# A router of two token tiles side by side: weights in halves of the array, tokens moving, logits turned once

## The chip, the cores and the metric

The kernel runs on one core of a Trainium2 chip. The metric is the device time in microseconds (us); three runs of the kernel before gave 1886.5, 1886.94 and 1890.55 us, with a median of 1886.94. The engines are PE (TensorE, with its weight loads listed apart as PEld), DVE (VectorE), ACT (ScalarE), POOL (GpSimd) and SP (SyncE, which here issues DMAs).

## The reference, cut to what matters

A decoder layer over x of 32 x 64 tokens of 512 numbers in float32: self attention of 32 heads of 128, a cross attention over the channels, and a mixture of biases of 64 experts, each behind a layer norm and each added to x. The change lies in the last:

```
def _L0_ffn_ref(hidden_states, router_weight, router_bias, expert_bias):
    K_TOP = 8
    ...
    flat = hidden_states.reshape(T, H)
    logits = jnp.einsum('th,eh->te', flat, router_weight) + router_bias
    scores = jax.nn.softmax(logits, axis=-1)
    topk_w, topk_idx = jax.lax.top_k(scores, K_TOP)
    w_sum = topk_w.sum(axis=-1, keepdims=True)
    w_dense = jnp.zeros((T, E), dtype=scores.dtype).at[jnp.arange(T)[:, None], topk_idx].add(topk_w)
    bias_mix = jnp.einsum('te,eh->th', w_dense, expert_bias)
    out = flat * w_sum + bias_mix
...
x = x + _L0_attn_ref(_layernorm(x, axis=-1), ...)
x = x + _L0_xattn_ref(_layernorm(x, axis=-1), ctx_1024, ...)
x = x + _L0_ffn_ref(_layernorm(x, axis=-1), ...)
```

T is 2048 tokens, H is 512 and E is 64.

## The kernel before, in words

The tokens are cut into 16 tiles of 128 (NT), so that a tile holds its tokens in the 128 partitions. The kernel has two phases. In the first, up to about 1400 us, the attention runs over groups of two heads (the functions of `HeadGroup` and `Window`, lines 363 to 815). In the second the attention's output is multiplied with Wo, two tiles (a pair) at a time, in seven products per pair instead of eight (`strassen_out`, line 947); a product is 16 matmuls of 128x256 on PE (`chunks`, line 847), and after every four of them the function yields.

At each yield the main loop calls `advance` (line 1449), which takes one step of every tile that has left the attention. Such a tile goes through `after_attention` (line 1187): first `cross_attention` (line 1057), then `experts` (line 1126). Both are generators; the number that they yield says how many further steps of four matmuls are let pass before they go on. So the work of a tile's tail is strewn between the output products of the next pair, and PE's order is exactly the order in which the code issues it (`manual_schedule` of PE, line 67). In this second phase the order of DVE, ACT, POOL and SP is not written out: the framework's scheduler chooses it, and the tile pools decide when a buffer may be written again.

The names that matter below:

- `transposed` (line 246) turns the four 128x128 blocks of a tile with four PE transposes (line 253), into PSUM.
- `experts`: layer norm `xn`; `ft`, the turned tile, copied from PSUM by ACT (line 1131); `pl`, the logits of 128 tokens by 64 experts, four matmuls that hold a block of 128 tokens as the weights and let the 64 columns of `rwt` stream (line 1135); `lg`, the logits with the bias (line 1139); `top`, `neg`, `ex`, `den`, `inv`, `rest`, `chosen`, the choice of the best eight and the softmax, on DVE, with the exponential on ACT (lines 1140 to 1153); `wd`, the dense weights, and `ws`, their sum (lines 1162 and 1164); line 1166 adds the tile times `ws` to x.
- Two tiles share one `wds`, and the second of them goes on: `pw` turns the dense weights of both at once (line 1173), `wt` is ACT's copy of it, `pm` is their product with the expert biases (line 1182), and line 1184 adds it to x, which is then stored. The last two tiles, 14 and 15, each go alone (`alone`).
- `cross_attention`: `kv` (lines 1067 and 1068), the energies `e` (line 1077: rows 0 to 63 and 64 to 127 of the array by turns), the softmax `probs` on DVE and ACT, `att` (line 1107, one buffer), their turned form, and `py` (lines 1112 and 1114, the latter into partitions 0 to 63 and 64 to 127 by turns), added at line 1122.
- `s` (line 559) are the scores of the first phase; they go to the two halves of the output partitions by turns.
- In the last pair of `strassen_out` (line 978) lines 1012, 1015 and 1016 add the last products to tile 15; line 229 is the statistics of a layer norm; lines 1024 to 1038 and 983 to 985 are DVE's sums over a whole block of 128x2048; lines 1042, 1045 and 1046 add products to `p1` and `p17`.

Of the kernel before, what the change touches and what calls it, by code (L numbers as in the profile page):

```python
# [8 lines left out]
F32 = mybir.dt.float32  # L9
AF = mybir.ActivationFunctionType  # L10
ALU = mybir.AluOpType
AX = mybir.AxisListType

P = 128
NB, SEQ, D = 32, 64, 512
NT = NB * SEQ // P
KC = D // P
# [11 lines left out]
NEXP = 64  # L29
# [12 lines left out]
def decoder_layer(  # L42
# [23 lines left out]
    nc = tc.nc  # L66
# [3 lines left out]
    small = ctx.enter_context(tc.tile_pool(name="small", bufs=4))  # L70
# [5 lines left out]
    ps_a = ctx.enter_context(tc.tile_pool(name="ps_a", bufs=3, space=bass.MemoryType.PSUM))  # L76
    ps_t = ctx.enter_context(tc.tile_pool(name="ps_t", bufs=2, space=bass.MemoryType.PSUM))
    ps_s = ctx.enter_context(tc.tile_pool(name="ps_s", bufs=3, space=bass.MemoryType.PSUM))
# [95 lines left out]
    def load_x(t, place=None):  # L174
# [9 lines left out]
        for q in range(NQUAD)  # L184
    ]

    ident = const.tile([P, P], F32, tag="ident", name="ident")
# [6 lines left out]
            name=nc.get_next_instruction_name(),  # L194
# [45 lines left out]
    def layernorm(xt, name):  # L240
        ((mean, rstd),) = statistics([xt], name, True)
        xn = work.tile([P, D], F32, tag="xn", name=f"xn_{name}", bufs=3)
        nc.vector.tensor_scalar(xn, xt, mean, rstd, ALU.subtract, ALU.mult)
        return xn

    def transposed(src, name, pool=None):

        if pool is None:
            pt = ps_t.tile([P, 4, P], F32, tag="pt", name=f"pt_{name}")
        else:  # L250
            pt = pool.tile([P, 4, P], F32, tag="ps", name=f"pt_{name}")
        for j in range(4):
            nc.tensor.transpose(pt[:, j, :], src[:, j, :], ident)  # L253
        return pt
# [869 lines left out]
    chosen_by = {}  # L1124

    def experts(t, xt):
        name = f"f{t}"
        xn = layernorm(xt, name)
        yield 3
        ft = work.tile([P, KC, P], F32, tag="ft", name=f"ft_{name}", bufs=1)  # L1130
        nc.scalar.copy(ft, transposed(xn.rearrange("p (kc k) -> p kc k", k=P), name))
        yield 1
        pl = ps_s.tile([P, NEXP], F32, tag="ps", name=f"pl_{name}")
        for kc in range(KC):
            nc.tensor.matmul(  # L1135
                pl, ft[:, kc, :], rwt[:, kc, :], start=kc == 0, stop=kc == KC - 1
            )
        lg = work.tile([P, NEXP], F32, tag="lg", name=f"lg_{name}")
        nc.vector.tensor_tensor(lg, pl, rb_b, ALU.add)
        top = small.tile([P, 8], F32, tag="top", name=f"top_{name}")  # L1140
        nc.vector.max(top, lg)
        neg = small.tile([P, 1], F32, tag="neg", name=f"neg_{name}")
        nc.vector.tensor_scalar(neg, top[:, 0:1], -1.0, None, ALU.mult)
        ex = work.tile([P, NEXP], F32, tag="ex", name=f"ex_{name}")
        den = small.tile([P, 1], F32, tag="den", name=f"den_{name}")
        nc.scalar.activation(ex, lg, AF.Exp, bias=neg, accum_out=den)
        inv = small.tile([P, 1], F32, tag="inv1", name=f"inv1_{name}")
        nc.vector.reciprocal(inv, den)

        rest = work.tile([P, NEXP], F32, tag="rest", name=f"rest_{name}")  # L1150
        nc.vector.match_replace(rest, top, lg, -3e38)
        chosen = work.tile([P, NEXP], F32, tag="chosen", name=f"chosen_{name}")
        nc.vector.tensor_tensor(chosen, lg, rest, ALU.not_equal)

        alone = t >= NT - 2
        side = 0 if alone else t % 2
        if side:
            wds, other = chosen_by.pop(t - 1)
        else:
            wds = work.tile([P, 2, NEXP], F32, tag="wds", name=f"wds_{name}")  # L1160
        wd = wds[:, side, :]
        nc.vector.scalar_tensor_tensor(wd, ex, inv, chosen, ALU.mult, ALU.mult)
        ws = small.tile([P, 1], F32, tag="ws", name=f"ws_{name}")
        nc.vector.tensor_reduce(ws, wd, AX.X, ALU.add)

        nc.vector.scalar_tensor_tensor(xt, xn, ws, xt, ALU.mult, ALU.add)
        if not alone and not side:
            chosen_by[t] = wds, xt
            return
        yield 3  # L1170
        n = NEXP if alone else 2 * NEXP
        pw = ps_t.tile([P, P], F32, tag="pt", name=f"pw_{name}")
        nc.tensor.transpose(pw[0:n, :], wds.rearrange("p a e -> p (a e)")[:, 0:n], ident)
        wt = work.tile([P, P], F32, tag="wt", name=f"wt_{name}")
        nc.scalar.copy(wt[0:n, :], pw[0:n, :])
        yield 1

        both = [(t, xt)] if alone else [(t - 1, other), (t, xt)]
        pms = [ps_a.tile([P, D], F32, tag="pa", name=f"pm{i}_{name}") for i in range(len(both))]
        for i, pm in enumerate(pms):  # L1180
            rows = slice(i * NEXP, (i + 1) * NEXP)
            nc.tensor.matmul(pm, wt[rows, :], eb_sb[rows, :], start=True, stop=True)
        for (at, it), pm in zip(both, pms):
            nc.vector.tensor_tensor(it, it, pm, ALU.add)
            nc.sync.dma_start(out=out_flat[bass.ts(at, P), :], in_=it)

    def after_attention(t, xt):
        second = t % 2 and t < NT - 1
        if second:
            yield 0  # L1190
        yield from cross_attention(t, xt, 3 if second else 1)
        yield from experts(t, xt)
# [13 lines left out]
    work = phase.enter_context(tc.tile_pool(name="attention", bufs=2))  # L1206
# [303 lines left out]
    work = ctx.enter_context(tc.tile_pool(name="output", bufs=2, reuse_waits="tile"))  # L1510
# [11 lines left out]
    rwt = work.tile([P, KC, NEXP], F32, tag="rwt", name="rwt", bufs=1)  # L1522
    load_beside(rwt, rw_t.rearrange("(kc p) e -> p kc e", p=P))
    rb_b = work.tile([P, NEXP], F32, tag="rb", name="rb_b", bufs=1)
# [76 lines left out]
```

## Time and profile before

| what | value |
| --- | --- |
| median of three runs | 1886.94 us |
| the profiled execution's own time | 1888.35 us |
| its span on the core | 1886.6 us |
| busy PE, share of the span | 1856.9 us, 98% |
| busy weight loads | 1613.8 us, 86% |
| busy DVE | 1259.9 us, 67% |
| busy ACT | 653.0 us, 35% |
| busy POOL | 1014.8 us, 54% |
| instructions | 40521 |

The span is the time from the first to the last instruction of the profiled execution; its own time has what lies around that. Busy times of PE are modelled where matmuls overlap, so the distance between two starts says more of a matmul's cost than its length does. "L1135 x8" in a row means eight instructions of line 1135; a float32 matmul appears as two passes, each with a weight load of its own. "128*64 128x128" is the part of the array in use (rows*columns) and what streams through it. An arrow to the left, as in "<-DVE xn_x L243", names what ended an engine's idle time.

### The profile page before, as it was taken

The numbers are of one execution on the slowest core, as the hardware profiler recorded it, in microseconds if no ns is written. First come the engines' busy times: TensorE is split into PE (matmuls) and PEld (weight loads), VectorE is DVE, ScalarE is ACT, GpSimd is POOL, SyncE is SP. The second block draws the span as 40 slices with busy tenths as digits, with TensorE's granted clock in tenths as the row PEclk, the third lists the DMA queues.
The fourth block names the chain that finished last, engine by engine and source line by source line (L and its number), as shares of the span: only waits on it lengthen the run. The fifth ranks groups of instructions, "written<-read, shape, count | busy, mean of one in ns | idle before, by whom it ended". The sixth has DMA issues, their size and how long they took to land.

```text
span 1886.6 us, 40521 instructions
## 1 busy us (share of the span) xinstructions
PE 1856.9 (98%) x16838; PEld 1613.8 (86%) x16838; DVE 1259.9 (67%) x2110; ACT 653.0 (35%) x1573; POOL 1014.8 (54%) x856
## 2 busy tenths in 40 slices
PE   9999999999999999999999999999999999999996
PEld 8888888888888888888888888888887888888884
DVE  6867777776777758776677677766684535554544
ACT  2344444344433443344433443443312211221122
POOL 5856776775667649776667767666241221121120
PEclk9999999999999999999999999999999999999997
DMA  4244434333443343333443333344844232223100
GB/s 141 68 132 145 129 121 128 124 108 124 127 131 104 113 147 102 113 102 114 131 129 113 113 113 102 102 135 135 299 137 154 70 114 80 80 71 115 45 26 23
DMA packets 164648, 215.04 MB, mean 114 GB/s; under 512 B 10160, under 2 KB 135152, under 8 KB 160368
## 3 DMA queue, kind: packets, MB, share of 16 engines
q1 hardware_dynamic: 157648, 206.62, 34.2%
q10 hardware_dynamic: 6816, 5.83, 1.0%
q8 instruction: 132, 2.16, 0.5%
q14 instruction: 52, 0.43, 0.1%
HBM read 172.05 MB, written 40.37 MB: 113 GB/s over the span
## 4 chain that ended last, share of the span: by engine, by line
PE 88%; DVE 5%; DMA 3%; POOL 2%; issue 1%; ACT 1%; ACTq 0%; SPq 0%; POOLq 0%; DVEq 0%
PE p_w L659 32%; PE py L852 17%; PE va L391 11%; PE vb L391 8%; PE ms_w L794 3%; PE o L596 3%; PE s L559 3%; PE pt_p L253 1%; PE pa L449 1%; PE e_x L1077 1%; PE py_x L1114 1%; PE py_x L1112 1%; PE pl_f L1135 1%; PE pt_x L253 1%; DMA rs<-row_w 1%
## 5 line engine op out<-in xcount | busy, mean ns | idle before, releaser
L659 PE MATMUL p_w<-x,w 128*128 128x256 f32 x2940 | 721.0, 382 | 3.6 <-DVE qk L670 2.9
L659 PEld LDWEIGHTS p_w<-x,w 128*128 128x128 f32 x2940 | 521.4, 190 | 60.2 <-DVE qk L670 2.4
L391 PEld LDWEIGHTS va<-w,x 128*128 128x128 f32 x2048 | 268.6, 192 | 13.0
L670 DVE TENSOR_TENSOR qk<-p_w,qk 128x512 f32<-128x512 f32 x360 | 213.1, 599 | 87.4 <-PE p_w L659 84.5
L391 PE MATMUL va<-w,x 128*128 128x128 f32 x2048 | 269.9, 275 | 0.0
L407 ACT COPY v<-va 128x256 f32<-128x256 f32 x256 | 96.2, 376 | 495.8 <-PE va L391 495.6
L683 DVE TENSOR_TENSOR qk<-p_w,qk 128x512 f32<-128x512 f32 x360 | 219.7, 620 | 40.5 <-PE p_w L659 36.8
L120 POOL TENSOR_TENSOR w<-w 128x768 f32<-128x768 f32 x126 | 243.9, 1946 | 2.4
L269 POOL TENSOR_TENSOR prob<-prob,inv 128x512 f32<-128x512 f32 x64 | 79.0, 1235 | 300.7 <-DVE inv L268 297.5
L546 POOL TENSOR_TENSOR qk<-qk,rs 128x512 f32<-128x512 f32 x128 | 177.8, 1390 | 105.9 <-DMA rs<-row_w 91.2
L852 PE MATMUL py<-wo,a 128*128 128x256 f32 x992 | 226.9, 381 | 0.0
L360 ACT ACTIVATE sq<-qk 128x512 f32<-128x512 f32 x256 | 161.4, 631 | 183.5 <-DVE qk L683 65.2
L852 PEld LDWEIGHTS py<-wo,a 128*128 128x128 f32 x992 | 184.3, 190 | 33.1 <-issue 8.7
L391 PEld LDWEIGHTS vb<-w,x 128*128 128x128 f32 x1536 | 201.4, 192 | 9.7
L391 PE MATMUL vb<-w,x 128*128 128x128 f32 x1536 | 202.4, 275 | 0.0
L548 DVE SCALAR_TENSOR_TENSOR qk<-qk,gqk,rs 128x512 f32<-128x512 f32 x128 | 181.6, 1419 | 4.2 <-DMA rs<-row_w 3.9
L852 PE MATMUL py<-wo_t,a 128*128 128x256 f32 x672 | 155.3, 382 | 0.0
L852 PEld LDWEIGHTS py<-wo_t,a 128*128 128x128 f32 x672 | 124.3, 190 | 17.6 <-issue 1.6
L976 POOL TENSOR_TENSOR x<-x,p 128x256 f32<-128x256 f32 x42 | 42.8, 1039 | 169.6 <-ACT p L1029 72.6
L411 DVE TENSOR_TENSOR v<-vb,v 128x256 f32<-128x256 f32 x192 | 80.8, 421 | 55.8 <-ACT v L407 28.6
L739 POOL TENSOR_TENSOR qk<-qk 128x256 f32<-128x256 f32 x120 | 102.8, 857 | 10.5 <-DVE qk L683 5.8
L261 DVE TENSOR_REDUCE mx<-s 128x8 f32<-128x512 f32 x64 | 44.1, 689 | 95.1 <-PE s L559 94.9
(191 smaller groups left out, 2256.7 us busy)
## 6 DMA issues: line engine op xcount, KB each, us to landing
rs<-row_w SPq DMA_DIRECT2D x120, 512.0 KB
mixed<-ot SPq DMA_DIRECT2D x64, 512.0 KB
a<-mixed SPq DMA_DIRECT2D x32, 1024.0 KB
w<-in_wq_dram SPq DMA_DIRECT2D x64, 256.0 KB
w<-in_wk_dram SPq DMA_DIRECT2D x62, 256.0 KB
w<-in_wv_dram SPq DMA_DIRECT2D x62, 256.0 KB
x<-in_x_dram SPq DMA_DIRECT2D x20, 256.0 KB
rs<-row SPq DMA_DIRECT2D x8, 512.0 KB
```

Of the source, the lines that this page charges most:

```text
L120: on.tensor_tensor(*(it.rearrange("p c j d -> p (c j) d") for it in (out, a, b)), ALU.subtract)
L360: nc.scalar.activation(sq, of, AF.Square)
L391: nc.tensor.matmul(to[:, j, :], left[i][:, c, j, :], right[i][:, c, 2, :], start=first and j == 0 and c == 0, stop=c == 1, skip_group_chec ...
L407: nc.scalar.copy(self.v[h, ab], what)
L411: nc.vector.tensor_tensor(it, what, it, ALU.add)
L546: nc.gpsimd.tensor_tensor(k, k, rk, ALU.mult)
L548: lambda: nc.vector.scalar_tensor_tensor(q, q, gqk, rq, ALU.mult, ALU.mult)
L659: nc.tensor.matmul(bank[:, s, :], self.w.inner[o][i], inner_x[self.half, o][i], start=first and s == 0, stop=True, skip_group_check=True,)
L670: nc.vector.tensor_tensor(to(t, j), bank, add(t, j), ALU.add)
L683: nc.vector.tensor_tensor(to(t, j), bank, to(t, j), ALU.add)
L739: on.tensor_tensor(to, to, what, ALU.add)
L852: nc.tensor.matmul(py, a[:, g, :], b[g // KH][:, g % KH, :], start=n == 0 and g == 0, stop=n == last and g == NHG - 1,)
```

## The change

For tiles 0 to 13 the router of a pair is made as one. Both turned tiles stand in one tile `fts`, which takes the single buffer of the tag `att`. The first tile of a pair ends after its copy into `fts`. The second one lets the router's weights (128x64 per block) stand in the array as weights, in columns 0 to 63 for the first tile and 64 to 127 for the second, and the 128 tokens of each stream: `plt` holds the logits of both tiles, with the experts in the partitions. ACT copies it to `lgt`, and four output matmuls later one PE transpose brings it to `pl`, 128 tokens by 2 x 64. One DVE instruction adds the bias for both. The choice, the softmax, `ws` and the update of x are as before, for the first and the second tile in turn, both behind this point. The number yielded before `pw` is 2 instead of 3, and one step of 0 is new before the transpose. Tiles 14 and 15 keep the former router. The pools `lg` and `wds` hold one or two tiles' worth.

```diff
         xn = layernorm(xt, name)
         yield 3
-        ft = work.tile([P, KC, P], F32, tag="ft", name=f"ft_{name}", bufs=1)
+
+        alone = t >= NT - 2
+        if alone or t % 2 == 0:
+            fts = work.tile([P, 2, KC, P], F32, tag="att", name=f"ft_{name}", bufs=1)
+        else:
+            fts, x_a, xn_a = chosen_by.pop(t - 1)
+        ft = fts[:, 0 if alone else t % 2, :, :]
         nc.scalar.copy(ft, transposed(xn.rearrange("p (kc k) -> p kc k", k=P), name))
         yield 1
-        pl = ps_s.tile([P, NEXP], F32, tag="ps", name=f"pl_{name}")
-        for kc in range(KC):
-            nc.tensor.matmul(
-                pl, ft[:, kc, :], rwt[:, kc, :], start=kc == 0, stop=kc == KC - 1
-            )
-        lg = work.tile([P, NEXP], F32, tag="lg", name=f"lg_{name}")
-        nc.vector.tensor_tensor(lg, pl, rb_b, ALU.add)
...
+        if alone:
+            tiles = [(t, xt, xn)]
+            pl = ps_s.tile([P, 1, NEXP], F32, tag="ps", name=f"pl_{name}")
+            for kc in range(KC):
+                nc.tensor.matmul(
+                    pl[:, 0, :], ft[:, kc, :], rwt[:, kc, :], start=kc == 0, stop=kc == KC - 1
+                )
+        elif t % 2 == 0:
+            chosen_by[t] = fts, xt, xn
+            return
         else:
-            wds = work.tile([P, 2, NEXP], F32, tag="wds", name=f"wds_{name}")
...
-        nc.vector.scalar_tensor_tensor(xt, xn, ws, xt, ALU.mult, ALU.add)
-        if not alone and not side:
-            chosen_by[t] = wds, xt
-            return
-        yield 3
-        n = NEXP if alone else 2 * NEXP
+            tiles = [(t - 1, x_a, xn_a), (t, xt, xn)]
+
+            plt = ps_s.tile([P, P], F32, tag="ps", name=f"plt_{name}")
+            for kc in range(KC):
+                for side in range(2):
+                    nc.tensor.matmul(
+                        plt[side * NEXP : (side + 1) * NEXP, :],
+                        rwt[:, kc, :],
+                        fts[:, side, kc, :],
+                        start=kc == 0,
+                        stop=kc == KC - 1,
+                    )
+            lgt = work.tile([P, P], F32, tag="wt", name=f"lgt_{name}")
+            nc.scalar.copy(lgt, plt)
+            yield 0
+            pl = ps_s.tile([P, 2, NEXP], F32, tag="ps", name=f"pl_{name}")
+            nc.tensor.transpose(pl.rearrange("p a e -> p (a e)"), lgt, ident)
+        n = len(tiles)
+        lgs = work.tile([P, n, NEXP], F32, tag="lg", name=f"lg_{name}")
+        nc.vector.tensor_tensor(
+            lgs, pl, rb_b.unsqueeze(1).to_broadcast([P, n, NEXP]), ALU.add
+        )
+        wds = work.tile([P, n, NEXP], F32, tag="wds", name=f"wds_{name}")
+        for side, (at, x_, xn_) in enumerate(tiles):
+            lg = lgs[:, side, :]
...
+            wd = wds[:, side, :]
+            nc.vector.scalar_tensor_tensor(wd, ex, inv, chosen, ALU.mult, ALU.mult)
+            ws = small.tile([P, 1], F32, tag="ws", name=f"ws{side}_{name}")
+            nc.vector.tensor_reduce(ws, wd, AX.X, ALU.add)
+
+            nc.vector.scalar_tensor_tensor(x_, xn_, ws, x_, ALU.mult, ALU.add)
+        yield 3 if alone else 2
+        n *= NEXP
         pw = ps_t.tile([P, P], F32, tag="pt", name=f"pw_{name}")
...
```

More of the change, by code (lines that the diff above doesn't have):

```diff
@@ L1134, in experts @@
-        for kc in range(KC):
-            nc.tensor.matmul(
-                pl, ft[:, kc, :], rwt[:, kc, :], start=kc == 0, stop=kc == KC - 1
-            )
-        lg = work.tile([P, NEXP], F32, tag="lg", name=f"lg_{name}")
[L1139 to L1158, printed above, removed]
-        else:
-            wds = work.tile([P, 2, NEXP], F32, tag="wds", name=f"wds_{name}")
[L1161 to L1164, printed above, removed]
@@ new lines, in experts @@
+        n = len(tiles)
[6 more added lines that the diff above has]
+            lg = lgs[:, side, :]
+            top = small.tile([P, 8], F32, tag="top", name=f"top{side}_{name}")
+            nc.vector.max(top, lg)
+            neg = small.tile([P, 1], F32, tag="neg", name=f"neg{side}_{name}")
+            nc.vector.tensor_scalar(neg, top[:, 0:1], -1.0, None, ALU.mult)
+            ex = work.tile([P, NEXP], F32, tag="ex", name=f"ex{side}_{name}")
+            den = small.tile([P, 1], F32, tag="den", name=f"den{side}_{name}")
+            nc.scalar.activation(ex, lg, AF.Exp, bias=neg, accum_out=den)
+            inv = small.tile([P, 1], F32, tag="inv1", name=f"inv1{side}_{name}")
+            nc.vector.reciprocal(inv, den)
+            rest = work.tile([P, NEXP], F32, tag="rest", name=f"rest{side}_{name}")
+            nc.vector.match_replace(rest, top, lg, -3e38)
+            chosen = work.tile([P, NEXP], F32, tag="chosen", name=f"chosen{side}_{name}")
+            nc.vector.tensor_tensor(chosen, lg, rest, ALU.not_equal)
+            wd = wds[:, side, :]
[3 more added lines that the diff above has]
+            nc.vector.scalar_tensor_tensor(x_, xn_, ws, x_, ALU.mult, ALU.add)
@@ L1176, in experts @@
         yield 1
-        both = [(t, xt)] if alone else [(t - 1, other), (t, xt)]
-        pms = [ps_a.tile([P, D], F32, tag="pa", name=f"pm{i}_{name}") for i in range(len(both))]
+        pms = [ps_a.tile([P, D], F32, tag="pa", name=f"pm{i}_{name}") for i in range(len(tiles))]
         for i, pm in enumerate(pms):
@@ L1182, in experts @@
             nc.tensor.matmul(pm, wt[rows, :], eb_sb[rows, :], start=True, stop=True)
-        for (at, it), pm in zip(both, pms):
+        for (at, it, _), pm in zip(tiles, pms):
             nc.vector.tensor_tensor(it, it, pm, ALU.add)
```

## The prediction

> **What bounds the kernel now.** I read the chain of waits first, then the table of stretches, then TensorE's (PE's) waits in the part that the change touches (1426 us to the end), last the timeline around the router.
>
> ```profile
> PE 88%; DVE 5%; DMA 3%; POOL 2%; issue 1%; ACT 1%; ACTq 0%; SPq 0%; POOLq 0%; DVEq 0%
> ```
>
> ```profile
> 1675.00:1737.00 62.00, 62.00 (x324) 51.00 (x323) 30.95 (x63) 11.67 (x47) 12.21 (x16) 1.00 0.26 88
> ...
> 1851.00:1887.00 36.00, 20.00 (x80) 11.43 (x78) 15.52 (x43) 8.00 (x29) 2.71 (x6) 0.70 0.08 29
> ```
>
> ```profile
> PE pt_f L253 <- DVE inv_x L1103: 3.7, 1, 3.7
> PE pt_f L253 <- DVE xn_f L243: 2.7, 1, 2.7
> PE e_x L1077 <- DVE xn_x L243: 2.2, 1, 2.2
> PE kv L1067 <- DMA ct<-in_ctx_dram: 1.9, 1, 1.9
> ```
>
> The columns of a stretch are length, busy PE, weight load, DVE, ACT, POOL, granted clock, DMA share and GB/s. One period of the output stage (two tiles, some 62 us) has PE busy all 62.00 us while DVE has half its time free. The largest waits are single events, the first three in the last 36 us, where tiles 14 and 15 run alone and DVE's and ACT's latencies set the pace. So a microsecond taken from PE in tiles 0 to 13 is a microsecond of the kernel, as long as nothing makes PE wait; and work moved near 1851 can lengthen the tail.
>
> **The change, part by part.** PE records from two answers of the timeline (start, length, with the drain of the last pass inside the length, so I go by starts):
>
> ```profile
> 1832.11 1.00 PE L1135 MATMUL pl_f<-rwt,ft_f 128*128 128x64 f32 x8
> ...
> 1832.94 1.95 PE L852 MATMUL py<-wo_t,a 128*128 128x256 f32 x8
> ...
> 1837.34 1.89 PE L852 MATMUL py<-wo_t,a 128*128 128x256 f32 x8
> ```
>
> ```profile
> 1389.03 3.62 PE L852 MATMUL py<-wo_t,a 128*128 128x256 f32 x16
> 1392.58 1.15 PE L559 MATMUL s<-qk 128*64 128x64 f32 x32
> 1393.66 1.16 PE L596 MATMUL o<-probt,v 64*64 64x64 f32 x64
> ...
> 1437.60 1.89 PE L852 MATMUL py<-wo_t,a 128*128 128x256 f32 x8
> 1439.42 1.16 PE L1077 MATMUL e_x<-kvs,xn_x 64*128 64x128 f32 x16
> 1440.51 5.45 PE L852 MATMUL py<-wo_t,a 128*128 128x256 f32 x24
> 1445.79 1.04 PE L253 MATMUL pt_x<-ident,prob_x 128*128 128x128 f32 x8
> 1446.67 5.35 PE L852 MATMUL py<-wo,a 128*128 128x256 f32 x24
> ```
>
> *Removed: the router's L1135.* A float32 matmul is two passes, so a tile has 8. From 1832.11 to 1832.94 is 0.84 us unrounded, and the L852 group behind it lasts 1.95 instead of 1.89, its first pass 0.06 late: 0.89 us a tile, 1.79 us a pair. A pass streams only the 64 expert columns but loads 128 columns of tokens, and comes every 0.11 us, as long as a pass that streams 128.
>
> *Added: `plt`.* 4 x 2 matmuls, 16 passes of 128 moving columns, two halves of the array side by side. The same count and width stands in the trace, with halves of rows instead of columns: e_x at 1439.42. L852 before it needs 8 x 0.216 = 1.73 us, to 1439.33, so 0.09 us pass before it starts; it takes 1.09 us to the next start; and that L852 group lasts 5.45 against 5.35, 0.10 us late. In all 1.28 us. Single passes show pairs 0.112 us apart, the two of a pair 0.007 apart: the halves overlap. Column halves stand in the s block of L559: 32 passes of 64 columns in 1.08 us, pairs 0.058 apart, and its first weight load shows 0.05 instead of 0.10 us, with 64 columns to load. So plt: 0.09 in, 0.05 first load, 8 x 0.112 = 0.90, 0.10 out, 0.10 late start behind: 1.24 us. Bounds: 0.87 (8 x 0.109, the pace of transposes at 1445.79, edges hidden) and 2.13 (16 x 0.112 plus the same 0.34, no overlap). I take 1.24, because both tiled rows have all four edges.
>
> *Added: one transpose of the logits*, 0.88/8 = 0.11 us (1445.79 to 1446.67). Its ACT copy `lgt` (0.27 us, the row of wt at L1175) is behind nothing late, and 4 output matmuls (1.73 us) lie between; gone, that cover would cost up to 0.3 us a pair.
>
> *Sum on PE:* 1.79 - 1.24 - 0.11 = 0.44 us a pair, times 7 pairs (tiles 14 and 15 keep the old form) = 3.1 us. Bounds 7 x (1.79 - 0.87 - 0.11) = 5.7 gained, 7 x (2.13 + 0.11 - 1.79) = 3.2 lost.
>
> *Moved: the first tile's router waits for the second's.* DVE gets both at once, from the transposed logits on. Count from the end of plt: logits at 1.73 + 0.31 = 2.0 us (0.31 as from pw's start to wt's in the trace). In most pairs L1045 and L1046 of product 6 (0.42 each) are queued ahead, so 2.7. One router takes 1.70 us on DVE from lg to ws:
>
> ```profile
> 1840.10 0.23 DVE L1139 TENSOR_TENSOR lg_f<-pl_f,rb_b 128x64 f32<-128x64 f32 x1 [2.83 <-PE pl_f L1135]
> ...
> 1841.80 0.22 DVE L1164 TENSOR_REDUCE ws_f<-wds_f 128x1 f32<-128x64 f32 x1
> ...
> 1850.19 0.42 DVE L1015 TENSOR_TENSOR x<-x,py 128x256 f32<-128x256 f32 x1 [1.64 <-PE py L852]
> ...
> 1851.24 0.69 DVE L1184 TENSOR_TENSOR x<-x,pm_f 128x512 f32<-128x512 f32 x1 [0.30 <-PE pm_f L1182]
> ```
>
> Two in full succession end at 2.7 + 3.4 = 6.1; PE asks for them (pw) after 1.73 + 0.11 + 12 x 0.43 = 7.0. Cover 0.9 us, so nothing; beyond it, each tenth late costs 0.7 us over 7 pairs. xn of tile 0 is held longer (3 buffers), which only moves the next pair's second xn behind its update, many us before its e_x.
>
> *Last pair.* Here both routers meet tile 14's softmax on DVE. Its last prob is ready between 9.8 us (independent instructions start some 0.08 before the last ends, as 1841.80 to 1841.94 in the trace) and 11.4 (all in succession) after plt; L1015 was asked for at 10.3 and may slip 0.3, the idle time ahead of L1184 at 1851.24. So the tail starts 0 to 0.7 us late; I take 0.2. *Shared buffer.* `fts` now takes att's single buffer: tile 15's att copies wait for pl of tile 14 (1867.9 instead of 1865.4), two of 0.59 end at 1869.1, and their reader L1114 started at 1869.41: covered by 0.3, which is also the cost if the rows ahead of it run at the full clock. Against that, tile 15's statistics now precede tile 14's residual update (0.75 us) on DVE: up to 0.3 us gained, I take 0.2. Net of the tail 0, bounds -0.3 and +1.0.
>
> *Total:* -3.1 us. The profiled execution reads 1888.35 us, 1.75 around its span of 1886.6; the median of the runs, 1886.94, is 1.41 lower. The profiled time becomes 1885.2, the median **1883.8 us**.
>
> **Rivals.**
> *Weight loads shown.* If each pair of passes waited for its weights, as the first of the s block does (0.106 against 0.058), plt would cost 8 x 0.05 less the one counted, 0.34 us more: 0.10 a pair left, 0.7 us in all, 1886.2. The 0.058 of all later pairs speaks against it. Chance 0.07. [...]
>
> *Edges hidden.* plt at 0.87 to 0.95: 7 x 0.75 = 5.3 us gained, 1881.7. For it: plt's load could be pulled ahead. Against: 0.09 and 0.10 at every tiled block above. Chance 0.20, the nearest case that gains more. [...]
>
> *Halves in turn.* plt at 2.13: 3.2 us lost, 1890.1. Both tiled rows speak against it. Chance 0.05.
>
> *DVE late at pw (the slower side).* If one DVE pass of 2.3 us over 2048 columns (L1024 to L1038 in the trace) came to stand ahead of the double router, pw would wait 6.1 + 2.3 - 7.0 = 1.4 us in each pair: 9.8 - 3.1 = 6.7 us lost, 1893.6. It decides from 7.4 us after plt on, where the wait eats the 0.44. For it: the burst is bunched, ACT's two exponentials stand between its halves. Against: in the changed program's DVE queue those passes stand before the statistics of the router's input. Chance 0.08.
>
> **How the numbers follow.** The forecast has 0.60; its own range is 1882.8 to 1885.5 (the tail's bounds, and 0.1 us a pair either way on plt). A measurement of this kernel tells about 0.2%, 3.8 us, from no change: faster means below 1883.2. A quarter of the forecast (0.15) and the hidden edges (0.20) lie there: 0.35. Slower: DVE late (0.08) and part of halves in turn (0.02): 0.10. The rest, 0.55, is within 0.2%. The range leaves out the late DVE, the halves in turn and the far end of hidden edges: 1881.0 to 1887.6.
>
> **What would show it.** Right: 16 plt passes in pairs some 0.112 us apart, about 1.24 us from the end of the work before to L852 at pace, pl a lone pass of 0.11, PE busy without a break in tiles 0 to 13, and the chain still on PE. Wrong: pairs 0.16 apart (loads shown), passes 0.11 apart singly (in turn), waits of pw for wds or of pl for lgt, or L1015 of the last pair starting more than 0.5 us after its product.

## The result and the profile after

| | before | after |
| --- | --- | --- |
| median (22 runs each) | 1888.78 us | 1884.76 us |
| ratio after to before, 95% interval | | 0.9976 [0.9969, 0.9983] |
| span of the profiled execution | 1886.6 us | 1883.3 us |
| busy PE | 1856.9 us | 1854.0 us |

The changed kernel is faster by 0.24% (interval 0.17% to 0.31%); of 1888.78 us that is 4.5 us (3.2 to 5.9), while the two medians lie 4.0 apart. Between the two traces it is 3.3 us.

The chain of waits of the changed kernel, then its stretches (the same columns as before):

```profile
PE 89%; DVE 4%; POOL 3%; DMA 3%; issue 1%; ACT 1%; SPq 0%; POOLq 0%; DVEq 0%; ACTq 0%
```

```profile
1675.00:1737.00 62.00, 62.00 (x327) 50.45 (x326) 30.28 (x62) 12.64 (x54) 11.75 (x16) 1.00 0.25 88
1851.00:1884.00 33.00, 18.50 (x66) 9.87 (x66) 13.55 (x39) 6.45 (x26) 2.21 (x5) 0.65 0.06 24
```

PE is still busy all 62 us of a period, so nothing that moved made it wait. PE's waits from 1426 us to the end say the same:

```profile
PE pt_f L253 <- DVE inv_x L1103: 3.7, 1, 3.7
PE e_x L1077 <- DVE xn_x L243: 2.2, 1, 2.2
PE pt_f L253 <- DVE xn_f L243: 2.1, 1, 2.1
PE pw_f L1198 <- DVE wds_f L1190: 1.8, 1, 1.8
...
PE kv L1067 <- DMA ct<-in_ctx_dram: 0.7, 1, 0.7
```

There is no row in which `pw` waits for a pair's `wds`, or `pl` for `lgt`: the one wait of `pw`, of 1.8 us, is that of tile 15 at 1876.68 us, which goes alone, and the kernel before has it too, with 1.8 us at 1879.97. Of the rows above, two became smaller, the DMA's (1.9 to 0.7, differing from execution to execution, as shown below) and `xn_f`'s (2.7 to 2.1, which the shared buffer did).

The router of one pair, as PE ran it:

```profile
1528.11 1.09 PE L1155 MATMUL plt_f<-ft_f,rwt 128*64 128x128 f32 x16
1529.13 1.99 PE L852 MATMUL py<-wo_t,a 128*128 128x256 f32 x8
1530.96 0.27 PE L1166 MATMUL pl_f<-ident,lgt_f 128*128 128x128 f32 x1
1531.07 5.35 PE L852 MATMUL py<-wo,a 128*128 128x256 f32 x24
1536.26 0.27 PE L1198 MATMUL pw_f<-ident,wds_f 128*128 128x128 f32 x1
```

`plt` runs from 1528.11 to 1529.13; the last matmul before it is followed after 0.309 us instead of 0.216 (0.093 in), the first one behind it lasts 0.483 instead of 0.382 (0.101 late). These two are the edges of the block that the prediction counted; with the 1.024 between the starts, `plt` costs 1.218 us. The starts of its 16 passes are 7, 153, 7, 102, 7, 102, 7, 102 ... ns apart: two at a time, the pairs 0.109 apart (the first 0.160, with the first weight load). `pl` costs 0.109.

To separate the pairs from all else I cut each trace at three starts: the first `kv`, the `pw` of the seventh pair, the end. Starts and differences in us; the last column is the mean of the four pairs that lie between the second and the sixth `pw`, the quietest part:

| trace | to the first `kv` | `kv` to last `pw` | from there on | one pair |
| --- | --- | --- | --- | --- |
| before | 1428.43 | 419.72 | 38.41 | 61.69 |
| after | 1428.73 | 416.55 | 38.01 | 61.23 |
| after, three further executions | 1427.49, 1427.57, 1425.66 | 416.59, 416.55, 416.55 | 36.30, 37.48, 38.01 | 61.23 each |

The pairs give 3.13 to 3.17 us in each of the four traces, 0.45 a pair. The parts before and behind them differ by up to 3 us among executions of one program.

### The profile page after: what moved, and what is told of

Same layout as the page of the kernel before. It is cut to its first block, busy times and chain, and to the rows that moved or that the text cites. A ratio compares the mean times of both kernels' runs of the same rounds, so it can differ in the third digit from the quotient of the medians.

```text
span 1883.3 us, 40546 instructions
## 1 busy us (share of the span) xinstructions
PE 1854.0 (98%) x16845; PEld 1606.6 (85%) x16845; DVE 1253.5 (67%) x2103; ACT 653.7 (35%) x1580; POOL 1013.2 (54%) x856
## 4 chain that ended last, share of the span: by engine, by line
PE 89%; DVE 4%; POOL 3%; DMA 3%; issue 1%; ACT 1%; SPq 0%; POOLq 0%; DVEq 0%; ACTq 0%
PE p_w L659 32%; PE py L852 19%; PE va L391 11%; PE vb L391 8%; PE o L596 3%; PE ms_w L794 3%; PE s L559 3%; PE pt_p L253 1%; PE pa L449 1%; PE py_x L1114 1%; PE e_x L1077 1%; PE pt_x L253 1%; PE py_x L1112 1%; POOL w L120 1%; PE pb L449 1%
```

## The experiments

All variants start from the changed kernel unless it is said otherwise; each was timed together with the kernel before. Where a duration of a pair is given, it is the last column of the table above.

**1. The changed kernel again** (no edit).

> The changed kernel itself, as a yardstick beside the others. Theory 'PE time' (7 pairs, each 1.79 us of old router against 1.22 us of plt and 0.11 us of transpose): pairs 0.45 us shorter each, 3.2 us less between the first kv and the last pw of a pair than before, whatever the run. Rival 'something beyond PE' (the tail's order, a buffer): the median falls by 4 us or more again while the pairs in the trace give only 3.2.

Measured: 1884.32 us, ratio 0.998 [0.9968, 0.9991]. The pairs repeat to 0.03 us, the rest does not: the first `kv` came 0.94 us before that of the kernel before, though nothing that the change touches runs ahead of it, and the part behind the pairs was 2.1 us shorter. The median fell by 4.4 us while the pairs give 3.1, which is what the rival of the expectation named: something outside the pairs counts too (see *Total* below).

**2. One half of the array after the other.** Same 16 passes, other order:

```diff
-            for kc in range(KC):
-                for side in range(2):
+            for side in range(2):
+                for kc in range(KC):
```

> Undoes the alternation alone: all eight passes of the first half of the array are issued, then all eight of the second; the same 16 passes, weights and data. Theory 'side by side': matmuls start in order, so only neighbours overlap; plt takes 16 x 0.112 + 0.34 = 2.1 us, 0.9 us a pair more than the changed kernel, 6.3 us in all, and the kernel is some 2 to 3 us slower than before. Rival 'each half has a queue of its own': the second half's passes overtake the first's, plt stays at 1.22 us and the time at the changed kernel's.

Measured: 1888.56 us, ratio 0.9993 [0.9982, 1.0004]. A pair takes 61.72, 0.03 more than before: the whole gain is gone. In the timeline of this variant:

```profile
1651.71 1.58 PE L1155 MATMUL plt_f<-ft_f,rwt 128*64 128x128 f32 x16
1653.22 1.99 PE L852 MATMUL py<-wo_t,a 128*128 128x256 f32 x8
```

1.51 us between the starts instead of 1.02, and with the edges 1.71. The distances of the 16 starts in ns tell why it is neither 1.2 nor 2.1:

```
160 110 109 109   6 103 57 52 57 52 57   109 109 110 109
```

Four passes run alone; then come seven distances of 6 to 103 ns, in which the last four passes of one half and the first four of the other overlap; then four run alone again. The pass that starts 6 ns behind the fifth one has a recorded length of 0.323 us, as the first pass of each half has in the changed kernel, against 0.272 to 0.273 of the others: so the second half began ahead of the sixth to eighth pass of the first. Why eight of the 16 passes overlap here and the other eight do not, the trace does not show. Of the two orders that were run, only the one by turns has the halves side by side from end to end, with 1.02 us between the starts.

**3. The old form at the new place.** Tokens as weights again, both tiles in one block where `plt` stands, DVE's burst as in the change, no turn of the logits:

```diff
-            for kc in range(KC):
-                for side in range(2):
+            for side in range(2):
+                for kc in range(KC):
...
-                        plt[side * NEXP : (side + 1) * NEXP, :],
-                        rwt[:, kc, :],
+                        pl[:, side, :],
                         fts[:, side, kc, :],
+                        rwt[:, kc, :],
...
-            nc.tensor.transpose(pl.rearrange("p a e -> p (a e)"), lgt, ident)
```

> Keeps the pairing, the place and the bunched choice of both tiles, and undoes the halves: tokens as weights, 16 passes into the logits, no copy, no transpose. Theory 'PE time': the block costs 16 x 0.112 = 1.79 us, as two old routers; the pairs last as long as before, and the kernel is within 0.5 us of before, the tail's order giving 0 to 0.5 us. Rival 'the pairing and DVE's order bring the gain': 2 us or more less than before although the block is as long.

Measured: 1888.31 us, ratio 0.9993 [0.9982, 1.0005]; a pair takes 61.69, what it took before, and the 16 passes with their late successor 1.79:

```profile
1650.44 1.89 PE L1155 MATMUL pl_f<-rwt,ft_f 128*128 128x64 f32 x16
1652.17 1.95 PE L852 MATMUL py<-wo_t,a 128*128 128x256 f32 x8
```

So the gain of a pair lies in the form of the matmuls alone; pairing the routers and bunching DVE's work is worth nothing there, and costs nothing.

**4. `plt` cut in two,** with four output matmuls between its halves, to price the edges of a tiled block:

```diff
             for kc in range(KC):
+                if kc == KC // 2:
+                    yield 0
```

> Cuts plt in two blocks of eight passes with four output matmuls between them; nothing else. Theory 'each tiled block pays its edges' (0.09 in, 0.05 first load, 0.10 out, 0.10 late start behind): one more set of 0.34 us a pair, 2.4 us more than the changed kernel, about 1 us less than before. Rival 'edges are a trait of the rows read, not of the block' (hidden when loads can be pulled ahead): less than 0.1 us a pair, no difference that shows.

Measured: 1885.73 us, ratio 0.9984 [0.9973, 0.9994]. A pair takes 61.58, 0.35 more than with one block. Each block of 8 passes takes 0.59 to its successor, with 0.09 in and 0.10 late:

```profile
1655.25 1.99 PE L852 MATMUL py<-wo_t,a 128*128 128x256 f32 x8
1657.17 0.66 PE L1157 MATMUL plt_f<-ft_f,rwt 128*64 128x128 f32 x8
1657.76 1.99 PE L852 MATMUL py<-wo,a 128*128 128x256 f32 x8
```

The edges are real and cost 0.35 us a block. The time itself says less: the median is 1.4 us above that of experiment 1, where 2.4 was expected. The additional step also moved the work around it: in this trace PE waited 1.3 instead of 0.78 us at `pm` of the first pair, with a granted clock of 0.76 from 1486 to 1500 us (see the last section), and 2.2 instead of 0.65 us for `prob_x` at an `e_x` near 1808 us.

**5. An own buffer for `ft` of tiles 14 and 15.**

```diff
-        if alone or t % 2 == 0:
+        if alone:
+            fts = work.tile([P, 1, KC, P], F32, tag="ft", name=f"ft_{name}", bufs=1)
+        elif t % 2 == 0:
```

> Gives the turned tiles 14 and 15 a buffer of their own again, so that tile 15's att copies no longer wait for the logits of tile 14; nothing else. Theory 'covered': the copies start some 1 to 2 us earlier in the trace, their reader L1114 does not, since PE reaches it after L1112; the time stays at the changed kernel's (within 0.3 us by the trace). Rival 'the shared buffer costs the tail': L1114 of tile 15 starts earlier against pl of tile 14, and 0.5 us or more is gained.

Measured: 1885.39 us, ratio 0.9981 [0.9971, 0.9991], pairs 61.23. ACT's copies in the tail, first with the own buffer, then as changed:

```profile
1863.34 0.58 ACT L1109 COPY att_x<-pt_x 128x512 f32<-128x512 f32 x1 [0.27 <-PE pt_x L253]
```

```profile
1863.59 1.07 ACT L1109 COPY att_x<-pt_x 128x512 f32<-128x512 f32 x2 [2.86 <-PE pl_f L1143]
```

With one buffer the copies do wait for `pl` of tile 14. But in both, L1114 follows L1112 of tile 15 after 1.95 us, so nobody waits for the copies. Something else differs: DVE's order behind it, which experiment 12 takes up.

**6. One half of the array,** both tiles streamed through it (8 passes of 256 columns), two transposes of 64 rows:

```diff
-                        plt[side * NEXP : (side + 1) * NEXP, :],
...
+                nc.tensor.matmul(
+                    plt, rwt[:, kc, :], fts[:, :, kc, :], start=kc == 0, stop=kc == KC - 1
+                )
```

> Keeps the router's weights in the array and the tokens moving, but not the halves: both tiles stream one after the other through the first 64 columns, 8 passes of 256, into 64 partitions; two transposes instead of one. Theory 'side by side makes the gain': the block takes 8 x 0.216 + 0.34 = 2.07 us and the transposes 0.22, together 0.50 us a pair more than the old routers: 3.5 us slower than before. Rival 'moving the tokens makes the gain' (wider passes hide the weight loads): no slower than before.

Measured: 1891.55 us, ratio 1.0023 [1.0012, 1.0035]. A pair takes 62.43, 1.20 more than changed and 0.75 more than before:

```profile
1652.98 1.94 PE L1154 MATMUL plt_f<-ft_f,rwt 128*64 128x256 f32 x8
1654.86 1.99 PE L852 MATMUL py<-wo_t,a 128*128 128x256 f32 x8
1656.78 0.34 PE L1162 MATMUL pl_f<-ident,lgt_f 64*128 64x64 f32 x2
1657.05 3.29 PE L852 MATMUL py<-wo,a 128*128 128x256 f32 x14
```

The block takes 1.87 plus 0.20 of edges, 2.07; the two small transposes are a tiled block too and cost 0.46 instead of 0.11. So the weights as such bring nothing: without the second half working at the same time the change is a loss.

**7. One block less:** `pm` of five pairs is set two steps back and the next pair's first `e` forward, so that the two stand back to back.

```diff
-        yield 1
+        early = t % 2 == 0 and 4 <= t < NT - 2
+        yield 0 if early else 1
...
-        yield apart
+        yield 0 if early else apart
...
-        yield 5
+        yield 7 if early else 5
...
-        yield 1
+        yield 3 if 3 <= t < NT - 4 else 1
```

> The changed kernel, with pm of the pairs 1 to 5 put off by two steps and the kv and e of the next pair's first tile brought forward by one and two, so that pm (rows of the array in halves) and e (the same split) are one block. Theory 'each tiled block pays its edges': one set of 0.3 to 0.39 us less in five pairs, 1.5 to 2 us less than the changed kernel by the trace (first kv to last pw). Rival 'given back': the stored tiles, and so the next tiles' loads, come 3.5 us later, and PE waits for them or for a PSUM bank: no gain or a loss.

Measured: 1885.02 us, ratio 0.9981 [0.9967, 0.9995]. A steady pair takes 60.83, 0.40 less than changed:

```profile
1543.42 1.13 PE L1207 MATMUL pm_f<-eb_sb,wt_f 64*128 64x512 f32 x4
1544.38 1.06 PE L1078 MATMUL e_x<-kvs,xn_x 64*128 64x128 f32 x16
1545.37 1.99 PE L852 MATMUL py<-wo,a 128*128 128x256 f32 x8
```

Two things took it back in this trace: one stretch between two `pw` got 1.68 us longer than with the change alone, with a granted clock of 0.88 from 1486 to 1500 us instead of 1.00 (see the last section), and the last one 1.57 us longer, because `e_x` is asked for there before DVE has the statistics:

```profile
PE e_x L1078 <- DVE mv_x L230: 2.8, 1, 2.8
```

**8. The same for four pairs,** without the one that the last pair follows:

```diff
-        early = t % 2 == 0 and 4 <= t < NT - 2
+        early = t % 2 == 0 and 4 <= t < NT - 4
...
-        yield 3 if 3 <= t < NT - 4 else 1
+        yield 3 if 3 <= t < NT - 6 else 1
```

> The version with pm beside e_x, now for four of the pairs only, and not where the last pair follows. In the trace of the one with five, a steady pair was 0.85 us shorter than before the change (0.40 shorter than with the change alone), and PE waited once, 2.8 us in the last pair, for the statistics in front of e_x of tile 14's pair. Theory: each tiled block costs its two edges, so one block less per pair is worth 0.40 us, and the wait came from asking for e_x two steps sooner where DVE was late. Expected: no such wait of 2.8, first kv to the last pw 4.0 to 5.0 us shorter than before the change (3.2 with the change alone), the median 1.6 us under the changed kernel's. Rival: the wait only moves to another pair or comes back as a wait of the last pair for something else; then first kv to the last pw is 3.2 us or less shorter.

Measured: 1884.36 us, ratio 0.9979 [0.9968, 0.999]. In the trace the theory holds: no wait of 2.8, a pair at 60.83, and 414.94 us from the first `kv` to the last `pw`, 4.78 under before and 1.61 under the changed kernel. The median did not follow.

**9. The changed kernel beside it.**

> The changed kernel as it is, beside the version above on the same chip. Theory: first kv to the last pw is 3.1 to 3.2 us shorter than before (0.45 a pair), as in both traces so far, and the ratio of the medians falls near 0.998; what differs beyond that is the first phase and the clock of the tail, which the change does not touch. Rival: a gain outside the pairs that comes back in each run, which would give 0.9975 or less again.

Measured: 1883.92 us, ratio 0.9977 [0.9966, 0.9988].

**10. and 11. Both once more,** on one chip.

> The version with pm beside e_x in four pairs again, beside the changed kernel on one chip, because its trace was 1.6 us shorter from the first kv to the last pw than the changed kernel's, and its median not (1884.36 against 1883.92 us, with intervals of some 2 us each). Theory: the saving is a saving of time, and the equal medians are scatter; then the median is 1 to 2 us under the changed kernel's of the same call. Rival: the tail, whose clock halves in windows of some 3.4 us that do not follow the program, gives it back; then the medians are within 0.5 us again, though the trace shows 4.6 to 4.9 us from the first kv to the last pw against the kernel before.

> The changed kernel beside it. Theory: first kv to the last pw 3.1 to 3.2 us shorter than before, the ratio near 0.998; the step from L1122 of tile 15 to its xn 3.15 us, against 3.63 before, as in the traces so far.

Measured: 1882.77 us, ratio 0.997 [0.9958, 0.9983], for the four pairs; 1883.95 us, ratio 0.9972 [0.9962, 0.9983], for the changed kernel. The expectation of experiment 9 named 0.9975 or less as the sign of a gain outside the pairs: 0.9977 there is just above it, 0.9972 here below. The median of the version with four pairs is 1.2 us below that of the changed kernel this time, as expected, and was 0.4 above it in experiments 8 and 9. Together, the version with four pairs has a mean of 1883.9 us in 23 runs, the changed kernel 1884.0 in the 55 of its four sets; the scatter of single runs is some 2 us, so the difference is known to about 1 us, and 1.6 is not in it.

The trace of this second execution shows 416.62 us between the first `kv` and the last `pw`, because the clock was down for some 3.4 us behind the first `kv` (1.68 us); its four steady pairs take 60.83 again. What takes the saving back goes with the clock: the mean granted clock is 0.9933 in these 23 runs and 0.9941 in the 55, and at equal clock the version with four pairs is 1.1 us faster (0.3 to 1.9; an estimate, worked out under *Total* below). Why its clock is lower stays open, so I do not call this version better than the changed kernel.

**12. The kernel before, with only the tail's shared buffer:**

```diff
+        tag = "att" if t >= NT - 2 else "ft"
-        ft = work.tile([P, KC, P], F32, tag="ft", name=f"ft_{name}", bufs=1)
+        ft = work.tile([P, KC, P], F32, tag=tag, name=f"ft_{name}", bufs=1)
```

> The kernel before, with its router as it was; only ft of tiles 14 and 15 takes att's single buffer, as in the change. With the change, tile 15's statistics came before tile 14's residual update on DVE, and from L1122 of tile 15 to its xn took 3.15 us instead of 3.63; with an own buffer for the last two tiles it took 3.63 again. Theory: the shared buffer alone makes this order (the scheduler sets the update back), and it is the part of the gain that the prediction put at 0.2. Expected: every pair as long as before, L1114 of tile 15 not delayed by the wait of att's copies, 3.15 us from L1122 to xn, the kernel 0.5 us faster (ratio near 0.9997). Rival: the order comes from the paired router; then 3.63. Second rival: what is measured beyond the pairs (about 1.3 us) is all from here; then the ratio is near 0.9993.

Measured: 1888.01 us, ratio 0.9998 [0.9986, 1.0009]; pairs 61.69. DVE in the tail, first of the kernel before, then of this one:

```profile
1870.56 0.69 DVE L1122 TENSOR_TENSOR x<-x,py_x 128x512 f32<-128x512 f32 x1 [0.70 <-PE py_x L1114]
1871.17 0.75 DVE L1166 SCALAR_TENSOR_TENSOR x<-xn_f,ws_f,x 128x512 f32<-128x512 f32 x1
1871.83 0.69 DVE L229 BATCH_NORM_STATS2 st_f<-x 128x6 f32<-128x512 f32 x1
...
1874.19 0.55 DVE L243 TENSOR_SCALAR xn_f<-x,mv_f,rs_f 128x512 f32<-128x512 f32 x1 [1.00 <-POOL rs_f L234]
```

```profile
1874.80 0.69 DVE L1122 TENSOR_TENSOR x<-x,py_x 128x512 f32<-128x512 f32 x1 [1.77 <-PE py_x L1114]
...
1875.54 0.68 DVE L229 BATCH_NORM_STATS2 st_f<-x 128x6 f32<-128x512 f32 x1
1876.14 0.73 DVE L1167 SCALAR_TENSOR_TENSOR x<-xn_f,ws_f,x 128x512 f32<-128x512 f32 x1
...
1877.96 0.55 DVE L243 TENSOR_SCALAR xn_f<-x,mv_f,rs_f 128x512 f32<-128x512 f32 x1
```

The statistics (L229) now stand ahead of tile 14's update, and from L1122 to `xn_f` it takes 3.16 instead of 3.63 us. The changed kernel has 3.15 to 3.16 in its four traces; with an own buffer (experiment 5) it is 3.63 again. So the buffer makes the order. In the chains of waits of the kernel before and of the changed one, the steps from L1122 to `xn_f` and on to PE's `pt_f` follow one another, so the 0.47 us lie on the path that decides. Experiment 2 has the same order, but 3.34 us: there L1208, which stands ahead of `xn_f` on DVE, waited 0.57 us for PE's `pm`. The timing itself, at 0.02% with an interval of 0.12% either way, can neither show 0.5 us nor exclude 1.3.

## Why the prediction was right, and where a size was off

*The bound.* Right: PE busy without a break in the steady pairs, and a microsecond of PE there was a microsecond of the trace: in experiment 4 the second block costs 0.35 us on PE and a pair is 0.35 longer, in experiment 6 the block costs 0.85 and the transposes 0.35 more, and a pair is 1.20 longer.

*Removed, 1.79.* Right: the old form in one block cost 1.79 (experiment 3).

*Added `plt`, 1.24.* Measured 1.218 us: 0.09 in, 0.05 for the first load, 8 x 0.109 instead of 8 x 0.112, and 0.20 behind. Of its bounds, 2.13 is about what the block costs with one half working (2.07 in experiment 6) and 0.87 was never near. The rival of shown weight loads would have had pairs 0.16 apart; they are 0.109 apart. In the trace each weight load behind the first two starts 0.11 us ahead of its pass, while the pair before it runs, and only the first load of the block shows, with 0.05 us. From 1.79 to 1.218 the matmuls of the logits, without the transpose, became 1.47 times as fast; of the 1.218, the edges and the first load are 0.35 together, and experiment 4 priced them apart, at 0.35.

*Added transpose, 0.11; `lgt` covered.* Right: 0.109, and no wait for `lgt`.

*Sum, 0.44 a pair, 3.1 us.* Measured 0.453, 3.17 us.

*Moved DVE burst, nothing.* Right with more room than thought: in the pair shown the last `wds` ends 5.6 us behind `plt` (forecast at most 6.1), and `pw` comes 7.1 behind it. The rival of a late DVE did not arise.

*Last pair, 0.2 late.* Too pessimistic. Tile 14's last `prob_x` was ready 9.9 us behind `plt`, the early end of the 9.8 to 11.4, as DVE's independent instructions overlap there (`ws` runs from 1841.59 to 1841.80 us, the second `wds` starts at 1841.72); L1015 came with its product:

```profile
1846.03 0.69 DVE L1104 TENSOR_TENSOR prob_x<-prob_x,inv_x 128x512 f32<-128x512 f32 x1
1847.32 0.42 DVE L1015 TENSOR_TENSOR x<-x,py 128x256 f32<-128x256 f32 x1 [0.59 <-PE py L852]
```

*Shared buffer, covered; earlier statistics, 0.2 gained.* The first right, the second too small: 0.47. These are two sides of one edit, as experiments 5 and 12 show. This is the step whose size was off: the tail's net of 0, with -0.3 as its best end, should have been about -0.5.

*Total.* The prediction's 3.1 us becomes 3.6 with the tail (3.17 + 0.47), a ratio of 0.9981. That lies inside the intervals of all four comparisons (0.9976, 0.998, 0.9977, 0.9972), at the upper side of most. Taken together, though, the means of the four sets differ by 4.8 us (4.0 to 5.5), so some 1.2 us are beyond that sum, and it is not scatter.

This rest goes with the clock, for which the prediction had no term. Each run on record has its mean granted clock: in the mean it is 0.9941 in the 55 runs of the changed kernel and 0.9929 in the 125 runs of the kernel before that have one. Among runs of one kernel, 0.001 less clock went with 1.3 us more time (a straight line through the 287 runs with a clock, with a level of its own for each kernel). By this line the change is worth 2.8 us at equal clock (2.3 to 3.3), an estimate that is nearer the 3.17 us of the pairs than the measured gain is (the 0.47 of the tail does not show in it). The variants fit it too: at equal clock, each to about 1 us, experiment 2 takes 3.6 us more than the changed kernel (by its pairs 7 x 0.49 = 3.4), experiment 3 takes 2.6 (3.2), experiment 4 takes 2.7 (2.4) and experiment 6 takes 7.4 (8.4). Why the runs of the changed kernel were granted more clock, no run shows.

The 1883.8 us itself started from a median of 1886.94 in three runs; in the 22 runs beside the change the kernel before had 1888.78, so that 1884.76 stands 0.96 above the forecast though the gain was larger. A base that was 1.8 us too low and a gain that was 0.9 us too small (4.0 between the medians) partly offset each other: that the two times lie so near is luck, and what bears the prediction out is the time of a pair.

## What to carry to other kernels

Price a tiled matmul block as passes plus two edges (here 0.35 us together, the first load included), and put the halves by turns in the program: one half after the other lost the whole gain here (61.72 us a pair, 61.69 before and 61.23 by turns). Read such a small gain from start to start in the traces, here 3.13 to 3.17 us in four traces, since each stretch of 3.4 us at half speed moved the time of a single execution here by 1.6 to 1.7 us, and compare the granted clock of the runs before a rest is put down to the change. A buffer shared to save room is also an edit of the scheduler's order: look at what moved behind it.

## What the runs showed of the hardware that was not expected

In some of these traces a wait of PE cost twice, in its own time and in the clock behind it. At the first `kv` PE waits for a DMA, up to 3.2 us. Where it waited up to 1.9, the granted clock stayed at 1.00 behind it (`1429.00:1440.00`); where it waited 2.2 (experiment 5) and 3.2 (experiment 10) it fell to 0.84 over the next 11 us, that is some 3.4 us at half speed, and it took 1.68 us longer to the first `pw`. Experiment 10 there, as a whole and then in two parts, and after it the changed kernel:

```profile
1429.00:1440.00 11.00, 11.00 (x57) 9.25 (x57) 7.57 (x10) 3.49 (x18) 0.42 (x1) 0.84 0.35 139
```

```profile
1429.30:1432.50 3.20, 3.20 (x11) 2.58 (x10) 3.01 (x3) 0.21 (x1) 0.12 (x1) 0.50 0.97 399
1432.80:1440.00 7.20, 7.20 (x46) 6.10 (x45) 4.26 (x8) 3.12 (x17) 0.00 (x0) 1.00 0.05 13
```

```profile
1429.00:1440.00 11.00, 11.00 (x68) 9.29 (x68) 8.94 (x10) 3.91 (x19) 1.27 (x2) 1.00 0.33 130
```

No length of the wait decides it, though. Behind the wait of `pm` in the first pair (0.78 us in every trace but that of experiment 4) experiments 7 and 12 show 0.88 from 1486 to 1500 us, and experiment 4, with a wait of 1.3 us, shows 0.76; the other eleven traces show 1.00. The wait of 2.8 us in experiment 7 left it at 1.00. In experiment 7, behind the short wait and then around the long one:

```profile
1486.00:1500.00 14.00, 13.22 (x60) 9.88 (x59) 8.92 (x14) 3.56 (x20) 4.17 (x2) 0.88 0.24 76
```

```profile
1790.00:1804.00 14.00, 13.30 (x85) 11.58 (x86) 10.42 (x19) 3.81 (x20) 4.58 (x5) 1.00 0.24 81
```

The tail has it as well. In all traces but that of experiment 4, `e_x` of tile 15 starts 6.75 us behind the seventh `pw`, after a wait of 2.2 us. In six of these thirteen the clock is at half speed for 3.4 us from 6.6 to 8.0 us behind that `pw` on, and `pt_f` of tile 14 follows 15.2 to 15.3 us behind it; in the other seven it follows after 13.7 us. Both traces with the former router (before, experiment 12) are among the six, and of the four of the changed kernel only that of experiment 9 is. So the tails of two single traces cannot be compared for what the change does. In these runs, an idle stretch of 0.8 to 3.2 us in a busy PE had a second price, of 1.6 to 1.7 us for each stretch of 3.4 us at half speed, that was paid or not, which is part of the scatter of 2 us between executions of one program.
